# Moving the last transposes, loads and stores in the closing units of a conditioned attention + causal convolution kernel

## The chip, the cores and the metric

One core of one Trainium2 chip. The metric is device time in microseconds (us) of one execution; lower is better. TensorE (PE) does the matrix products and the transposes, VectorE (DVE) and ScalarE (ACT) read its results from PSUM, GpSimd (POOL) adds and reduces in SBUF, and SyncE (SP) issues every DMA of this kernel from one queue, in order.

## What is computed

The inputs are x of 4 x 1024 x 1024, four condition rows and the weights, all in f32. Cut to its core, the reference is:

```python
xn = rms_norm(x, g_norm) * (1 + scale) + shift      # scale, shift = cond @ W_emb + b_emb
q, k, v = split(xn @ W_qkv)                         # 16 heads of 64
q, k = rms_norm(q, g_q), rms_norm(k, g_k)
o = softmax(q @ k.T / 8) @ v
x = x + o + o @ W_out
x = x + causal_conv1d(x, 4 taps from cond) + b      # depthwise
```

## The kernel before, in words

**Stages.** The four batches are cut into 16 *doubles*, each two pairs of heads of one batch. A double's q, k and v come from 28 *products* (line 589; 4 matrix products of 128 x 384 each, counted twice for f32), seven block products P1 to P7 in Strassen's manner, for four token tiles each. Their operands are sums of blocks of the activations (`Chunk`, lines 257 to 329, written to scrA by way of the "r" buffers) and of the weights (`Weights`, lines 479 to 511, four blocks k = 0 to 3 for each double of weights, written to scrB by way of the "ob" buffers). A *unit* is one pair of heads and one half (512) of the query rows; there are 64, p = 0 to 63. Unit p scores eight key tiles (L629), copies them to SBUF (ScalarE, L637), keeps a running maximum (VectorE, L646), reduces it over the partitions (GpSimd, L651), copies it into PSUM (L660), subtracts it (VectorE, L665), takes the exponential (ScalarE, L669) and adds the rows (GpSimd, L671). The values' product (L692) and the row sums (`finish`, L707) of unit p - 1 are written between the scores of unit p. The row sums go through DRAM to be spread and inverted (`spread` L725 to 730, `invert` L733 to 738), and `divide` (L747) writes the output of the pair to scrO.

**What fills a unit.** Between its scores a unit runs other pieces: seven steps T = 7(p+4) to 7(p+4)+6 of the list of products, the transposes of q and k (`transposes`, L459, with the copies kT and qT, L465 and L467), and output products. `split` puts the last 26 us of pieces (20 in the first 16 units) behind the unit's maximum. Products end at T = 447, in unit 59. The output of batches 0 to 2 is done by 70 block products (`Quad`, L881), of which the last two, g = 68 and 69, lie in unit 59; eight outputs of batch 2 (`REST`) are done plainly (`Out`) in units 60, 61 and 62, three, three and two; 16 outputs of batch 3 are last, seven of them (`own`) behind the last unit's maximum. An output is a residual (four transposes, L936), two products (L950, k = 0 to 3 and 4 to 7), a copy and an activation on ScalarE (L960, L974), three taps on VectorE (L986), four transposes (L997), a copy (L1001) and a DMA (L1002). `gather` (L770) loads a half of a batch's attention output from scrO in two transfers.

**Order.** TensorE, VectorE, ScalarE and GpSimd execute in the order in which the program is written. SyncE's queue is ordered by the compiler, so that a load can be issued well ahead of its place. The program keeps a planned clock: every piece has a planned time, `tick` adds it, and steps given to `defer` are written when the planned clock reaches their due time. `defer_gap` gives a step to the gap after a maximum instead: 2.7 us after a unit's `softmax`, `fill_gap` writes up to 6.5 us of them, scales of q and k first. `defer_quiet` moves a step that would fall into the exponentials to their end. `need(key)` writes the steps of a key at once: the transposes need the scale of their q and k (L450, L451), `load_w` of a block with summed weights needs all of a double's `combine`, and a product with the output weights needs the addition of the identity to them (`diagonal`, L930).

**Buffers.** Tag "m" is three PSUM tiles, for all products, transposes and row sums. "ob" (2) holds the operands of output products, "r" (2) the chunks, "x" (6) x, y, ot and squares, "wo" (3) output weights. `late` is the list of outputs whose transposes are still to come, with the planned time at which each was appended; `store(age)` writes those that are at least `age` old.

```python
PRODUCTS order: P1,P2 (8 steps), P6 (8-11), P7 (12-15), P4 (16-19), P5 (20-23), P3 (24-27)
LEADS = ((11, 7), (10, 9))     # [pair][half]: transposes so many steps behind the block's last product
R_HOME = ("r", 8, 2)
```

Of the kernel before, what the change touches and what calls it, by code (L numbers as in the profile page):

```python
# [21 lines left out]
def kernel(  # L22
# [33 lines left out]
    B, N, DIM = x.shape  # L56
    D = DIM // HEADS
    NJ = DIM // P
# [33 lines left out]
    clock = [0.0]  # L92
# [164 lines left out]
    class Chunk:  # L257
# [69 lines left out]
        def store(self):  # L327
            for src, i0, i1 in self.stores:
                nc.sync.dma_start(scrA[self.b][self.q][:, i0:i1, self.k, :], src)
# [149 lines left out]
    class Weights:  # L479
# [6 lines left out]
        def load(self):  # L486
            d, k = self.d, self.k
            self.b = {}
            four = apool.tile([P, 4, HN], F32, tag="ob", name=f"b_{self.name}", bufs=2)
            for kh in range(2):  # L490
                for y in range(2):
                    t = four[:, 2 * kh + y, :]
                    self.b[kh, y] = t[:, :W3]
                    for s, src in enumerate(w_block(kh, 2 * d + y, k)):
                        nc.sync.dma_start(t[:, s * P : (s + 1) * P], src)
            if d:
                if d > 1:
                    defer_gap(5.0, ("B", d), 2.5, self.combine)
                else:
                    defer_quiet(TO_B, ("B", d), self.combine)  # L500
# [18 lines left out]
    NPR = len(PRODUCTS)  # L519
# [238 lines left out]
    def gather(b, half):  # L758

        for kh in range(2):  # L760

            n = KH - kh if b == B - 1 else KH
            for k in range(n):
                need("oT", b, kh * KH + k, half)
            if half and b == B - 1:
                four = apool.tile([P, 8, QN], F32, tag="r", name=f"ob_{b}_{kh}_{half}", bufs=2)
                four = four.rearrange("p i t -> p (i t)").rearrange("p (k t) -> p k t", t=HN)
            else:
                four = apool.tile([P, KH, HN], F32, tag="ob", name=f"ob_{b}_{kh}_{half}", bufs=2)
            nc.sync.dma_start(four[:, :n, :], scrO[b][half][:, kh * KH : kh * KH + n, :])  # L770
            for k in range(n):
                oTs[b, kh * KH + k, half] = four[:, k, :]
# [240 lines left out]
    BEHIND = 26  # L1013
    SHARES = (0.25, 0.5, 0.25)
    LEADS = ((11, 7), (10, 9))
    DIVIDE = 18.0
    STEP_FIRST = 1.6
    BEHIND_FIRST = 20.0
# [2 lines left out]
    AGE = 30.0  # L1021
    LOUD = 5.0
    AGE_REST = 5.0
    W_AT = 3
    STORE = 30.0
    TO_B = 12.0
    P6_AT = 3
    STEPS_B = ((16, 19, 22, 25), (7, 12, 17, 22))
    outs, norms, chunks, weights, doubles, quads = {}, {}, {}, {}, {}, {}
    LAST = (B - 1) * 2 * NJ  # L1030
    NB = 2 * NJ
    ND = B * NJ // 2
# [3 lines left out]
    def piece(T):  # L1036


        n, i = divmod(T, NPR)
        pieces = []  # L1040
        free = lambda f: pieces.append((0.0, f))
        if i == 0 and n < ND and n not in doubles:
            free(lambda: doubles.__setitem__(n, Double(n)))

        for m in (n, n + 1):
            for name, at in WEIGHTS.items():
                if m == 0:
                    at = WEIGHTS_FIRST.get(name, NPR)
                elif m == 1 and name == "P6":
                    at = P6_AT  # L1050
                if m < ND and at + (m - n) * NPR == i:
                    free(lambda m=m, name=name: load_w(m, name))
        a = T // 2 + LOADS_A
        if T % 2 == 0 and 4 <= a < ND * NPR // 2:
            free(lambda: load_a(a))

        for name, (c, g) in ENDS.items():
            last = max(j for j, pr in enumerate(PRODUCTS) if pr[0] == name)
            for s, at in ((1, last + LEADS[c][g]), (0, last + LEADS[c][g] + 1)):
                m = n - at // NPR  # L1060
                if i == at % NPR and 0 <= m < ND:
                    pieces.append((0.45, lambda m=m, s=s, c=c, g=g: doubles[m].pairs[c].transposes(g, s)))
        if n < ND:
            b, d = divmod(n, PB)

            if b + 1 < B and d == PB - 2:
                if i == 0:
                    norms[b + 1] = Norm(b + 1, range(NT))
                if i % 3 == 0 and i < 24:
                    free(lambda: norms[b + 1].squares(i // 3))  # L1070
                if i == 26:
                    free(norms[b + 1].root)
            if b + 1 < B and (d == PB - 1 or d == PB - 2 and i == 27):
                s = (i + 1) // 3
                if i == 27 and d == PB - 2:
                    free(lambda: chunk_load(b + 1, 0))
                elif i % 3 == 1 and i < 24:
                    s = i // 3
                    free(lambda: chunk_load(b + 1, s + 1))
                    for c in range(2):  # L1080
                        pieces.append((0.45, lambda c=c: chunks[b + 1, s].transposes(c)))

            if b == 0 and d + 1 < PB and i in STEPS_B[d > 0]:
                free(lambda: Weights(d + 1, STEPS_B[d > 0].index(i)).load())

            if n in (PB - 1, PB) and i % 14 == W_AT:
                free(lambda: OutWeights((n - PB + 1) * 2 + i // 14).load())
            pieces.append((TIME, lambda: doubles[n].piece(i)))
        return pieces
# [21 lines left out]
    def out_load(m):  # L1111
        if m < B * NB and m not in outs:
            b, i = divmod(m, NB)
            outs[m] = Out(b, i % NJ, i // NJ)
            outs[m].load()

    def out_pieces(m):

        return [
            (0.0, lambda: out_load(m)),  # L1120
            (0.45, lambda: outs[m].residual()),
            (0.0, lambda: out_next(m)),
            (3.5, lambda: outs[m].product(0)),
            (3.5, lambda: outs[m].product(1)),
        ]

    NQ = 2 * KH + KH // 2
    NG = NQ * len(OUT)
# [7 lines left out]
    REST = [(B - 2) * NB + h * NJ + j for h in range(2) for j in (2, 3, 6, 7)]  # L1136
    REST_PLAN = {p: n for p, n in zip(range(B * NB - 4, B * NB - 1), (3, 3, 2))}

    def out_load_product(g):
        b, i = divmod(g, 4 * len(OUT))  # L1140
        j, i = divmod(i, len(OUT))
        if g < NG:
            if i == 0:
                quads[b, j] = Quad(b, j)
            quads[b, j].load(OUT[i])

    def out_product(g):
        b, i = divmod(g, 4 * len(OUT))
        j, i = divmod(i, len(OUT))

        def step():
            if g == 0:
                out_load_product(0)
            quad = quads[b, j]
            quad.product(OUT[i])
            if OUT[i] in quad.outs:
                late.append((clock[0], quad.outs[OUT[i]].store))
            out_load_product(g + 1)

        pieces = [(3.95 if OUT[i] in ("P2", "P3", "P7", "P4") else 3.5, step)]  # L1160
        return [(0.0, lambda: store(AGE))] + pieces
# [7 lines left out]
    def between(p):  # L1169

        b, i = divmod(p, NB)
        slots = [[] for _ in range(7)]
        for j in range(7):
            T = 7 * (p + 4) + j
            slots[j] = piece(T) if T < ND * NPR + max(LEADS[1]) + 2 else []
        slots[0].append((0.0, lambda: store(AGE)))
        d, k = divmod(p - 11, NB)
        if 0 <= d < B - 1 and k % 2 == 0 and k < NJ:
            slots[0].append((0.0, lambda: OutSums(d, k // 2).load()))
        for a, g in enumerate(range(products_until(p), products_until(p + 1))):  # L1180
            slots[(2, 5)[a]] += out_product(g)
        if p in REST_PLAN:
            at = sum(n for q, n in REST_PLAN.items() if q < p)
            for m in REST[at : at + REST_PLAN[p]]:
                if m in REST[:: len(REST) // 2]:
                    slots[6].append((0.0, lambda m=m: gather(B - 2, m // NJ % 2)))
                slots[6] += [(0.0, lambda: store(AGE_REST))] + out_pieces(m)
                slots[6].append((0.0, lambda m=m: late.append((clock[0], outs[m].store))))
        return [piece for slot in slots for piece in slot]
# [12 lines left out]
    def run(pieces):  # L1202
        for t, step in pieces:
            until = clock[0] + t
            step()
            if until > clock[0]:
                tick(until - clock[0])
# [33 lines left out]

    own = []
    for m in range(LAST, LAST + NJ - 1):
        own += out_pieces(m) + [(0.45, store), (0.0, lambda m=m: late.append((clock[0], outs[m].store)))]

    last = None
    for p in range(B * NB):
# [34 lines left out]
    last.finish()  # L1282
    last.divide()
    for m in range(LAST + NJ - 1, B * NB):
        run(out_pieces(m) + [(0.45, store)])
        late.append((clock[0], outs[m].store))
    store()

# [37 lines left out]
```

## Time and profile before

| what | value |
|---|---|
| median of 3 runs | 2920.79 us (2920.69 to 2922.56) |
| the profiled run | 2919.7 us |
| its span, first to last instruction | 2917.7 us |
| mean granted TensorE clock | 0.987 |
| DMA | 510.98 MB, mean 175 GB/s; 53.3% of 16 engines' span |

The page has six parts: busy time by engine, the span in 40 slices, DMA queues, the chain of work that ended last, the costliest groups of instructions, and the DMA issues. A group's line gives the line of the program, the engine, the operation, out<-in by name with shapes, the count, the busy time with the mean of one, and the idle time just ahead with what released it. A timeline gives start, duration, and instructions that follow one another, merged; a bracket holds the idle time ahead and its releaser. f32 matrix products are recorded as two instructions each, and the ends of TensorE's instructions are modelled, so that a duration overlaps the next start by some tenths of a us; the steps between starts are the safer measure.

In the chain of the whole span TensorE has 71%, VectorE 13%, ScalarE 7%, DMA 4% and unexplained issue 3%. TensorE's share of busy time in the 40 slices is 90% or more in all but the first (7 tenths) and two late ones (8 tenths).

### The profile page before, as it was taken

How to read it: one execution, taken by the hardware profiler on the slowest of the kernel's cores; microseconds unless marked ns; L12 is line 12 of the kernel's file. 1: busy time of each engine (PE TensorE's matmuls, PEld its weight loads, DVE VectorE, ACT ScalarE, POOL GpSimd, SP SyncE). 2: the span in 40 equal slices, each digit the busy share in tenths (PEclk: the TensorE clock that was granted, in tenths of full speed). 3: DMA queues.
4: the chain of work that ended last, by engine and by line, in shares of the span. 5: the costliest groups of instructions: out<-in, count | busy, mean ns of one | idle time of the engine just before them, and what ended most of it. 6: DMA issues, size and time to landing. Idle time of an engine off the chain costs nothing.

```text
span 2917.7 us, 32188 instructions
## 1 busy us (share of the span) xinstructions
PE 2797.4 (96%) x10529; PEld 1322.4 (45%) x10529; DVE 2183.2 (75%) x2652; ACT 1692.7 (58%) x2269; POOL 1347.7 (46%) x534
## 2 busy tenths in 40 slices
PE   7999999999999999999999999999999999998999
PEld 3544444444444444454444444445444444443344
DVE  3578877888878767787878777787877777687653
ACT  3165757765656666764656667675555656565532
POOL 1045555555455553544554455355455544553520
PEclk9999999999999999999999999999999999999999
DMA  7864555645444555764565556656555444433333
GB/s 280 270 211 139 166 171 176 220 157 177 159 156 162 202 178 188 231 205 161 175 213 168 172 177 202 208 193 208 169 176 189 163 139 135 161 120 109 101 105 115
DMA packets 416254, 510.98 MB, mean 175 GB/s; under 512 B 41888, under 2 KB 327896, under 8 KB 406360
## 3 DMA queue, kind: packets, MB, share of 16 engines
q1 hardware_dynamic: 416088, 508.93, 53.3%
q8 instruction: 84, 1.38, 0.2%
q14 instruction: 82, 0.67, 0.1%
HBM read 413.43 MB, written 95.40 MB: 174 GB/s over the span
## 4 chain that ended last, share of the span: by engine, by line
PE 71%; DVE 13%; ACT 7%; DMA 4%; issue 3%; POOL 1%; SPq 1%; DVEq 0%; ACTq 0%; POOLq 0%
PE pqkv_P L589 28%; PE pav L692 14%; PE s L629 13%; PE po L950 5%; DVE mx L646 4%; PE po_P L881 4%; PE po L881 3%; ACT sp L637 3%; DVE sp L665 2%; ACT sp L669 1%; PE qkt L459 1%; DVE y L986 1%; PE tot L707 1%; DMA rec<-scrR 1%; PE otp L997 1%
## 5 line engine op out<-in xcount | busy, mean ns | idle before, releaser
L589 PE MATMUL pqkv_P<-w_P,a 128*128 128x384 f32 x3504 | 1198.5, 493 | 30.8 <-issue 12.0
L671 POOL TENSOR_TENSOR sum<-sum,sp 128x1024 f32<-128x1024 f32 x384 | 958.1, 2495 | 73.2 <-ACT sp L669 43.1
L589 PEld LDWEIGHTS pqkv_P<-w_P,a 128*128 128x128 f32 x3504 | 652.5, 192 | 505.7 <-issue 93.1
L637 ACT COPY sp<-s 128x1024 f32<-128x1024 f32 x512 | 512.0, 1015 | 486.9 <-PE s L629 380.8
L646 DVE TENSOR_TENSOR mx<-mx,sp 128x1024 f32<-128x1024 f32 x384 | 514.6, 1340 | 166.2 <-ACT sp L637 137.8
L665 DVE TENSOR_TENSOR sp<-sp,mbp 128x1024 f32<-128x1024 f32 x512 | 604.9, 1213 | 15.4 <-ACT mbp L660 15.1
L669 ACT ACTIVATE sp<-sp 128x1024 f32<-128x1024 f32 x512 | 526.7, 1054 | 138.8 <-DVE sp L665 134.6
L651 POOL PARTITION_ALL_REDUCE mb<-mx x64 | 221.4, 3459 | 828.2 <-DVE mx L646 559.3
L629 PE MATMUL s<-qT,kT 64*128 64x512 f32 x2048 | 518.6, 623 | 34.3 <-ACT sp L637 22.6
L692 PE MATMUL pav<-sp,v 128*64 128x512 f32 x2048 | 472.4, 604 | 0.7 <-DVE oT L747 0.7
L671 POOL TENSOR_TENSOR sum<-sp,sp 128x1024 f32<-128x1024 f32 x64 | 151.3, 2364 | 497.3 <-ACT sp L669 240.4
L629 PEld LDWEIGHTS s<-qT,kT 64*128 64x128 f32 x2048 | 170.0, 186 | 333.2 <-issue 172.3
L986 DVE SCALAR_TENSOR_TENSOR y<-x,cols,y 128x512 f32<-128x512 f32 x192 | 249.4, 1303 | 61.2 <-ACT y L974 56.6
L692 PEld LDWEIGHTS pav<-sp,v 128*64 128x64 f32 x2048 | 136.8, 138 | 322.3 <-issue 312.1
L646 DVE TENSOR_TENSOR mx<-sp,sp 128x1024 f32<-128x1024 f32 x64 | 107.8, 1685 | 103.7 <-ACT sp L637 103.7
L608 DVE TENSOR_TENSOR qk<-u,pqkv_P 128x256 f32<-128x256 f32 x256 | 106.8, 417 | 83.0 <-PE pqkv_P L589 81.0
L950 PE MATMUL po<-ob,wo 128*128 128x512 f32 x352 | 159.6, 606 | 4.4 <-DMA ob<-scrO 4.4
L881 PE MATMUL po_P<-o_P,wq_P 128*128 128x512 f32 x320 | 144.0, 592 | 0.2 <-DVE u L610 0.2
L660 ACT COPY mbp<-mb 128x1024 f32<-128x1024 f32 x64 | 65.1, 1018 | 118.3 <-POOL mb L651 118.2
L451 DVE TENSOR_TENSOR qk<-qk,ms 128x1024 f32<-128x1024 f32 x64 | 124.5, 1945 | 2.2
L881 PE MATMUL po<-o_P,wq_P 128*128 128x512 f32 x240 | 108.0, 592 | 0.0
L437 ACT ACTIVATE sq<-qk 128x512 f32<-128x512 f32 x128 | 76.6, 627 | 48.7 <-DVE qk L608 48.7
(96 smaller groups left out, 1890.5 us busy)
## 6 DMA issues: line engine op xcount, KB each, us to landing
a<-scrA SPq DMA_DIRECT2D x215, 512.0 KB
w_P<-scrB SPq DMA_DIRECT2D x64, 768.0 KB
o_P<-scrS SPq DMA_DIRECT2D x40, 1024.0 KB
w_P<-in_L_cond_W_qkv_dram SPq DMA_DIRECT2D x144, 256.0 KB
o_P<-scrO SPq DMA_DIRECT2D x30, 1024.0 KB
scrA<-r SPq DMA_DIRECT2D x28, 896.0 KB
wq_P<-scrW SPq DMA_DIRECT2D x70, 256.0 KB
xc<-in_x_dram SPq DMA_DIRECT2D x64, 256.0 KB
```

What stands on the lines that cost most here:

```text
L589: nc.tensor.matmul(pm, (chunks[0, k].r(place) if a is None else a[:, k, :])[:, t % 2 * P : (t % 2 + 1) * P], w[:, k, :], start=(k == 0), s ...
L629: nc.tensor.matmul(ps[:, h, :], pr.kT[kt // HT][h * D : (h + 1) * D, kt % HT * P : (kt % HT + 1) * P], pr.qT[self.half][h * D : (h + 1) * ...
L637: nc.scalar.copy(sp, ps)
L646: nc.vector.tensor_max(self.mx, self.mx if kt > 1 else self.sp[0], self.sp[kt])
L651: nc.gpsimd.partition_all_reduce(self.mb.rearrange("p h q -> p (h q)"), self.mx.rearrange("p h q -> p (h q)"), P, bass_isa.ReduceOp.max,)
L665: nc.vector.tensor_sub(self.sp[kt], self.sp[kt], self.mb)
L669: nc.scalar.activation(sp, sp, AF.Exp)
L671: nc.gpsimd.tensor_tensor(self.sum, self.sum if kt > 1 else self.sp[0], sp, ALU.add)
L692: nc.tensor.matmul(self.pav[h * D : (h + 1) * D, :], self.pr.v[kt // HT][:, kt % HT, h * D : (h + 1) * D], self.sp[kt][:, h, :], start=(kt ...
L881: nc.tensor.matmul(pm, self.w[name][:, k, :], self.o[name][:, k, :], start=(k == 0 and name not in ("P2", "P3", "P4")), stop=(k == KH - 1),)
L950: nc.tensor.matmul(self.pm, self.w[kh][:, k % KH, :], oTs[b, k, half], start=False, stop=(k == NJ - 1),)
L986: nc.vector.scalar_tensor_tensor(self.y, self.x1[:, k : k + HN], cols[:, r : r + 1], self.y, ALU.mult, ALU.add)
```

## The change

It has four parts.

1. *First weights' sums.* For the second double of weights (d = 1), `combine` of blocks k = 2 and 3 is given to `defer_gap` (2.5 us each) instead of `defer_quiet` with 12 us. The loads of blocks 0 and 1 come at steps 14 and 17 of the first double instead of 16 and 19.
2. *Last pair's transposes.* For the last double alone (m = ND - 1), the transposes of the second pair's second half (after P5) come 12 steps behind the block, not 9: T = 455 and 456, slots 0 and 1 of unit 61, instead of T = 452 and 453, slots 4 and 5 of unit 60. The other leads are the same, and the limit of T becomes 464.
3. *Attention output.* The second half of batch 2, like that of batch 3, is loaded into the "r" buffers instead of "ob". Both halves' `gather` calls for batch 2, and the load of the first `REST` output, are written after product g = 69 in unit 59, instead of in units 60 and 61 ahead of the outputs that use them.
4. *Outputs' transposes.* In `own` and in the last loop, `store` takes only outputs at least 8.5 us old on the planned clock, where one output adds 7.45: an output's transposes are written after the second output behind it, not the first. The planned 0.45 of that piece is gone.
Apart from these, the loop over `s` and `m` in `piece` is another way to write the same leads.

```diff
             if d:
-                if d > 1:
+                if d > 1 or k > 1:
                     defer_gap(5.0, ("B", d), 2.5, self.combine)
                 else:
                     defer_quiet(TO_B, ("B", d), self.combine)
...
-            if half and b == B - 1:
+            if half:
                 four = apool.tile([P, 8, QN], F32, tag="r", name=f"ob_{b}_{kh}_{half}", bufs=2)
...
+    LEADS_LAST = ((11, 7), (10, 12))
...
+    AGE_OWN = 8.5
...
-    STEPS_B = ((16, 19, 22, 25), (7, 12, 17, 22))
+    STEPS_B = ((14, 17, 22, 25), (7, 12, 17, 22))
...
-            for s, at in ((1, last + LEADS[c][g]), (0, last + LEADS[c][g] + 1)):
-                m = n - at // NPR
-                if i == at % NPR and 0 <= m < ND:
-                    pieces.append((0.45, lambda m=m, s=s, c=c, g=g: doubles[m].pairs[c].transposes(g, s)))
+            for s in (1, 0):
+                for m in (n - 1, n):
+                    at = last + (LEADS_LAST if m == ND - 1 else LEADS)[c][g] + 1 - s
+                    if 0 <= m < ND and (n - m) * NPR + i == at:
+                        pieces.append((0.45, lambda m=m, s=s, c=c, g=g: doubles[m].pairs[c].transposes(g, s)))
...
             out_load_product(g + 1)
+            if g == NG - 1:
+                for half in range(2):
+                    gather(B - 2, half)
+                out_load(REST[0])
...
-            slots[j] = piece(T) if T < ND * NPR + max(LEADS[1]) + 2 else []
+            slots[j] = piece(T) if T < ND * NPR + 16 else []
...
-                if m in REST[:: len(REST) // 2]:
-                    slots[6].append((0.0, lambda m=m: gather(B - 2, m // NJ % 2)))
...
-        own += out_pieces(m) + [(0.45, store), (0.0, lambda m=m: late.append((clock[0], outs[m].store)))]
+        own += out_pieces(m) + [(0.0, lambda: store(AGE_OWN)), (0.0, lambda m=m: late.append((clock[0], outs[m].store)))]
...
-        run(out_pieces(m) + [(0.45, store)])
+        run(out_pieces(m) + [(0.0, lambda: store(AGE_OWN))])
         late.append((clock[0], outs[m].store))
```

## The prediction, made before the changed kernel was run

> **What bounds the kernel now.** I read the page first (shares, then the chain that ended last), then TensorE's timeline at both ends of the span, then VectorE's, ScalarE's, GpSimd's and SyncE's timelines around each gap found there.
>
> ```profile
> PE 2797.4 (96%) x10529; PEld 1322.4 (45%) x10529; DVE 2183.2 (75%) x2652; ACT 1692.7 (58%) x2269; POOL 1347.7 (46%) x534
> ```
>
> TensorE sets the time, so an edit is worth what it takes out of, or puts into, TensorE's gaps and slow stretches. TensorE's timeline over the last 300 us, columns start, duration, what, and in brackets the idle time ahead with its releaser:
>
> ```profile
> 2630.85 0.66 PE L997 MATMUL otp<-ident,y 128*128 128x128 f32 x4
> 2637.41 1.97 PE L459 MATMUL qkt<-ident,qk 128*128 128x128 f32 x8 [5.90 <-DVE qk L451]
> 2639.17 1.06 PE L997 MATMUL otp<-ident,y 128*128 128x128 f32 x4
> 2640.02 1.06 PE L936 MATMUL po<-ident,xc 128*128 128x128 f32 x4
> 2640.87 7.74 PE L950 MATMUL po<-ob,wo 128*128 128x512 f32 x16
> 2648.45 0.60 PE L936 MATMUL po<-ident,xc 128*128 128x128 f32 x4
> 2648.89 7.03 PE L950 MATMUL po<-ob,wo 128*128 128x512 f32 x16
> ...
> 2689.38 0.60 PE L936 MATMUL po<-ident,xc 128*128 128x128 f32 x4
> 2694.33 10.09 PE L950 MATMUL po<-ob,wo 128*128 128x512 f32 x16 [4.35 <-DMA ob<-scrO]
> ...
> 2806.16 1.09 PE L997 MATMUL otp<-ident,y 128*128 128x128 f32 x4 [3.52 <-DVE y L986]
> 2807.04 1.06 PE L936 MATMUL po<-ident,xc 128*128 128x128 f32 x4
> 2807.89 7.00 PE L950 MATMUL po<-ob,wo 128*128 128x512 f32 x14
> ```
>
> See three waits, each followed by work slower than its like: 8 transposes in 1.97 us (1.09 elsewhere), an output's product in 7.74 or 10.09 (7.03). The first waits for VectorE:
>
> ```profile
> 2628.07 7.86 DVE L646 TENSOR_TENSOR mx<-mx,sp 128x1024 f32<-128x1024 f32 x6
> 2635.85 0.25 DVE L450 RECIPROCAL ms<-ms 128x16 f32<-128x16 f32 x1
> 2636.13 1.23 DVE L451 TENSOR_TENSOR qk<-qk,ms 128x1024 f32<-128x1024 f32 x1
> ```
>
> The scale that the transposes force stands behind the unit's maxima. The fourth gap is in unit 0, on TensorE and then on VectorE:
>
> ```profile
> 162.72 0.60 PE L459 MATMUL qkt<-ident,qk 128*128 128x128 f32 x4
> 169.19 5.43 PE L589 MATMUL pqkv_P<-w_P,a 128*128 128x384 f32 x8 [5.86 <-issue]
> ```
>
> ```profile
> 150.12 0.56 DVE L510 TENSOR_TENSOR b<-b 128x384 f32<-128x384 f32 x1 [0.83 <-DMA b<-in_L_cond_W_qkv_dram]
> 152.54 1.74 DVE L510 TENSOR_TENSOR b<-b 128x384 f32<-128x384 f32 x3 [1.86 <-DMA b<-in_L_cond_W_qkv_dram]
> 154.20 3.88 DVE L646 TENSOR_TENSOR mx<-mx,sp 128x1024 f32<-128x1024 f32 x3
> ```
>
> "Issue" at 163 names no releaser; TensorE resumes at 169.19, just as VectorE ends the adds of product 30 (168.47 to 169.09), which free one of the three PSUM tiles "m". They stand behind the first shift, that behind the spread maximum (GpSimd 161.95 to 166.26, ScalarE's copy to 167.31), that behind the maxima, and those behind the sums of the fourth weight block, which wait for their DMA.
>
> **What the skill says.** "TensorE: Matmul & The Clock Gate", Part 1: an idle window of about 3.4 us halves TensorE's clock. Agrees: 8 transposes took 1.97 us after 5.90 idle and 1.09 otherwise, and a 1.75 us wait (at 95 us) shows no slowing. "SBUF — State Buffer", Who interferes with whom: a VectorE operation with two SBUF inputs and a GpSimd one that reads SBUF shut each other out. Agrees: three taps took 7.46 us beside GpSimd's sums, 2.33 alone. The clock page, Architectural detail: VectorE and ScalarE are strict FIFO; the queue behind the maxima above is that.
>
> **The change, part by part.**
>
> (1) First weights' sums. Blocks 2 and 3 of the second pair of heads' weights (4 subtractions each, 2.33 us) leave the scores' stretch for the gap after the maximum; the loads of blocks 0 and 1 start two products (5.2 us) sooner. Without the sums the maxima are bound by ScalarE's last copy (154.05) and VectorE: seven maxima of 1.24 and two reductions (1.27) from 146.73, with the waits for copies, end at 156.7, not 161.65. GpSimd 3.25 to 4.3, the copy 1.0: spread at 162. But VectorE now has 2 x 2.33 of sums, 1.5 of scale and up to 1.3 of waiting for GpSimd's port ahead of the shift: 156.7 + 7.5 = 164.2, not 167.34, so 3.1 sooner (4.4 without port waiting). TensorE's wait shrinks to about 3 us or less and perhaps its slow product (5.43 for 2.75) goes too; that would be 5.7 or more, but GpSimd's sums, which end at 192.85 just ahead of the row sums at 193.50, move by 3 to 4 only and cap it. **-3.5**; ends 0 and -8.5 (5.86 + 2.6). The stores and the load of w that follows them come some 8 us later on SP's queue; the load of a behind it lands near 171 for a use at 172, so it is just hidden; uncovered it costs about 1.
>
> (2) Last pair's transposes. Eight move from unit 60 to unit 61, their scale into unit 60's gap (1.5 us of VectorE, which is nearly idle from 2641 to 2650: free). From 2631.51 to the end of the first rest output at 2648.45 are 16.94 us; left are 0.44 + 0.44 + 6.87 = 7.75 (steps of the warm outputs). **-9.2**. What else it needs by then: y of the last product's output (taps end 2625.75) is ready; its w diagonal (2637.27 in VectorE's order) and x (issued 2634.03) are late for 2632, but part 3 loads that output in unit 59, so both move ahead of the maxima. Unit 60's later chain (copy of the maximum, shifts, exps, sums) hangs on this product's end through ScalarE's order and shifts with it. In unit 61 sixteen transposes stand in a row, then two outputs' transposes and a residual: seven PSUM tiles through three buffers at ScalarE's 0.53 to 0.59 a copy. The residual starts near 2683.1 instead of 2682.03: **+1.1**. New order: with 0.9 less on the planner's clock, the reciprocal of the row sums (L733) falls behind the first rest output's taps, as it does in unit 62 (2739.92): about 3 us later in its chain. Row reciprocals then land near 2650 for a division near 2651: hidden, 0 to +3.
>
> (3) Attention output. The second half of batch 2 gets the "r" buffers, idle since batch 3's chunks, instead of waiting for "ob". Its two 1 MB transfers leave 2687 to 2694, so 4.35 + (10.09 - 7.03) = **-7.4**. Next late is the next output's diagonal, behind taps and four shifts on VectorE: +0.2 to +0.5. I take **-7.2**. Batch 3's second half now waits for "r" until the last rest output (2740 and 2743.5), batch 3's first half can go into "ob" at 2686: at 2741 one 1 MB transfer, not 1.8 MB, runs beside the rec transfer (7.34 us) that the unit 63 stall hangs on: **-0.8**, ends -4 and +2 (a SyncE queue held longer by it).
>
> (4) Outputs' transposes. From 2802.5 to 2815.59 are 13.1 us where a warm step is 7.75: **-5.3**. One output later y is 7.4 us older (taps end 2806.0, next use 2809.9). At the end, one output's four transposes leave the last product's front for the wait on the last taps: **-0.4**. The "x" ring of 6 then holds y of three outputs, one ot and at most two x: just enough.
>
> Sum: -3.5 - 9.2 + 1.1 - 7.2 - 0.8 - 5.3 - 0.4 = **-25.3**. The profiled run took 2919.7 (span 2917.7 and 2.0 around it): 2894.4. The median stands 1.1 above it: **2895.5**.
>
> **Rivals.** (a) A new wait in unit 60 (chance 0.16): the late reciprocal holds SyncE's queue, the weights of the second rest output queue behind it, and its second product waits 4 us and runs cold, or unit 0 gives nothing. Of part 2 some 2 are left, or of part 1 none: 2899 to 2903. For it: in unit 60 SyncE now issues those weights (2645.70) right behind rec. Against: in unit 62, with that order, the weights went ahead. (b) More than I count (0.15): unit 0's whole stall, and rec no longer disturbed, its row sums' wait (1.96) gone: 2888 to 2891. (c) **Slower** (0.05): the second half's data is whole by about 1820, and batch 3's chunks still write "r" until 1934. If SyncE takes a buffer as soon as it is free (a transfer of batch 3 was issued at 2487.99, 255 us ahead of its place), the chunks have one buffer. One at 1851 holds it until its store at 1879, the next came at 1865: 14 us of wait and 3 cold; two such meetings are 34: 2895.5 + 34 = 2929. It decides from 25 us on. Against: x loads (2560.96, 2600.64) did not overtake tiles that engines write in their ring, while w loads, with a ring of their own, did. (d) The change doesn't act (0.04), TensorE's gaps being filled by others behind them: 2916 to 2921.
>
> **Numbers.** 2895.5 within 2891 and 2899: 0.60. Low 2889, high 2906, from the parts' ends and case (a). What a measurement here can tell from no change is about 0.2%, 5.8 us: below 2915 is faster. Faster 0.91, same 0.04, slower 0.05.
>
> **What would show it.** No wait on qk L451 and no DMA ob wait on TensorE; rest outputs at 7.03 each; no wait on y L986 but the last; sixteen qkt in unit 61; the wait at 163 at 3 us or less. Wrong if the rest outputs wait for wo, if chunks' transposes wait near 1860, or if row sums wait for GpSimd.

## The result, and the profile after

| what | before | after |
|---|---|---|
| median on the first chip, 6 runs each | 2919.65 us (2914.30 to 2922.56) | 2900.64 us (2891.97 to 2907.69) |
| ratio, with its 95% interval | 1 | 0.9937 (0.9915 to 0.9959) |
| median on a later chip, 11 and 6 runs | 2915.35 us (2909.45 to 2922.58) | 2895.52 us (2891.95 to 2900.84) |
| ratio there | 1 | 0.9933 (0.9918 to 0.9947) |
| the profiled run | 2919.7 us | 2907.69 us |
| its span | 2917.7 us | 2905.7 us |

The change is faster by some 18 to 20 us; the second interval is 15.5 to 23.9 us (0.0053 and 0.0082 of 2915). Predicted were 25.3 us less and a time of 2895.5. The profiled run of the first set was the slowest of its six, so its span is not compared as a whole below, but stage by stage.

**TensorE's timeline of the kernel after**, units 60 and 61, columns as before:

```profile
2636.72 0.64 PE L707 MATMUL tot<-sum,ones 128*32 128x256 f32 x8
2639.20 1.09 PE L997 MATMUL otp<-ident,y 128*128 128x128 f32 x8
2640.13 0.60 PE L936 MATMUL po<-ident,xc 128*128 128x128 f32 x4
2640.57 7.03 PE L950 MATMUL po<-ob,wo 128*128 128x512 f32 x16
...
2655.62 7.03 PE L950 MATMUL po<-ob,wo 128*128 128x512 f32 x16
2664.88 1.13 PE L629 MATMUL s<-qT,kT 64*128 64x512 f32 x4 [1.17 <-DVE sp L665]
...
2680.05 1.53 PE L459 MATMUL qkt<-ident,qk 128*128 128x128 f32 x12
2682.21 0.66 PE L459 MATMUL qkt<-ident,qk 128*128 128x128 f32 x4 [0.63 <-ACT kT L465]
...
2691.55 7.03 PE L950 MATMUL po<-ob,wo 128*128 128x512 f32 x16
```

The wait of 5.90 us for the scale and that of 4.35 us for "ob" are gone, and the rest outputs' products take 7.03 us (one, at 2699.29, 7.22). From the first transpose (2639.20) to the end of the third product's steps (2662.58, where a step is 6.96 as at 2730.97 to 2737.93) are 23.4 us, 32.7 before: the predicted 9.2 are there. One wait is new: the second pair of scores waits for VectorE's last shift. VectorE's timeline of the kernel after says why:

```profile
2662.47 1.23 DVE L930 TENSOR_TENSOR wo<-wo,ident 128x128 f32<-128x128 f32 x1 [2.26 <-DMA scrO<-oT]
2663.62 1.21 DVE L665 TENSOR_TENSOR sp<-sp,mbp 128x1024 f32<-128x1024 f32 x1
```

The shift stood behind the addition of the identity to the weights of the fourth rest output, ahead of which VectorE was idle for 2.26 us. This output is not used before unit 61. The addition waited for its weights: their load was issued at 2659.25, and the last wait on a semaphore ahead of it ended at 2662.4. (The bracket names another transfer; in the kernel with part 2 and the early load, below, it names the weights.) VectorE's timeline of the kernel before has the same addition behind the last shift, where nothing waited for it:

```profile
2661.10 2.34 DVE L665 TENSOR_TENSOR sp<-sp,mbp 128x1024 f32<-128x1024 f32 x2
2663.36 2.38 DVE L930 TENSOR_TENSOR wo<-wo,ident 128x128 f32<-128x128 f32 x1
```

The load was issued equally far ahead of the end of the third product in both kernels (3.3 us: 2660.26 of 2663.59, 2659.25 of 2662.58). So what changed is the place of the addition in VectorE's order, which follows the planned clock.

The first gap, in unit 0, is smaller but not gone. TensorE, then VectorE of the kernel after:

```profile
167.45 5.46 PE L589 MATMUL pqkv_P<-w_P,a 128*128 128x384 f32 x8 [3.23 <-issue]
```

```profile
158.11 6.15 DVE L510 TENSOR_TENSOR b<-b 128x384 f32<-128x384 f32 x8
164.18 0.25 DVE L450 RECIPROCAL ms<-ms 128x16 f32<-128x16 f32 x1
164.46 1.22 DVE L451 TENSOR_TENSOR qk<-qk,ms 128x1024 f32<-128x1024 f32 x1
165.61 1.21 DVE L665 TENSOR_TENSOR sp<-sp,mbp 128x1024 f32<-128x1024 f32 x1
```

The spread maximum was in PSUM at 162.83 (ScalarE's copy, 161.81 and 1.02 long). The shift began at 165.61, since the sums and the scale stood ahead of it: 2.8 us that the part costs itself.

At the end only the last four transposes still wait for their taps, as predicted, but twelve transposes now stand behind the last product, not eight, and eight in a row stand behind the first output of that stretch:

```profile
2834.22 1.04 PE L997 MATMUL otp<-ident,y 128*128 128x128 f32 x8
2835.75 0.66 PE L936 MATMUL po<-ident,xc 128*128 128x128 f32 x4 [0.48 <-ACT y L974]
...
2896.87 1.04 PE L997 MATMUL otp<-ident,y 128*128 128x128 f32 x8
2900.84 1.09 PE L997 MATMUL otp<-ident,y 128*128 128x128 f32 x4 [2.94 <-DVE y L986]
```

To count stage by stage I use the starts of the row sums (L707) of each unit on TensorE as marks: in the table and wherever a unit's time is given below, "unit 60" is from the row sums of unit 59 to those of unit 60, and so on; "end" is what follows those of unit 63. The same marks serve for all kernels below; times in us, each from one profile.

| kernel | start to the row sums of unit 1 | units 2 to 58 | 59 | 60 | 61 | 62 | 63 | end | 59 to end |
|---|---|---|---|---|---|---|---|---|---|
| before | 229.3 | 2354.7 | 44.3 | 48.5 | 48.6 | 40.6 | 72.6 | 79.1 | 333.6 |
| after | 227.6 | 2365.8 | 43.3 | 40.8 | 42.2 | 39.2 | 66.9 | 79.8 | 312.3 |
| after, second set | 228.7 | 2357.2 | 43.8 | 40.7 | 42.5 | 39.4 | 66.9 | 79.8 | 313.0 |
| part 1 alone | 224.9 | 2350.5 | 43.3 | 49.1 | 49.0 | 40.6 | 72.6 | 79.1 | 333.7 |
| parts 2 to 4 | 230.8 | 2354.4 | 43.2 | 41.1 | 42.3 | 39.2 | 66.8 | 79.8 | 312.4 |
| part 2 alone | 231.0 | 2353.9 | 43.3 | 51.0 | 46.4 | 40.0 | 73.9 | 78.7 | 333.3 |
| part 2 and the early output load | 229.1 | 2356.5 | 43.8 | 40.9 | 45.1 | 40.0 | 73.9 | 78.7 | 322.4 |
| parts 2 and 3 | 228.5 | 2352.9 | 43.2 | 40.8 | 42.3 | 39.7 | 73.0 | 79.1 | 318.0 |
| part 3 alone | 228.8 | 2355.2 | 43.4 | 49.0 | 41.1 | 39.2 | 73.7 | 78.9 | 325.2 |
| part 4 alone | 228.7 | 2351.3 | 43.7 | 49.1 | 46.6 | 40.0 | 66.8 | 79.4 | 325.7 |
| after, one sum in the gap | 224.9 | 2361.7 | 43.2 | 40.9 | 42.1 | 40.4 | 67.1 | 79.4 | 313.0 |
| after, reciprocal sooner | 226.9 | 2351.9 | 43.2 | 40.8 | 42.5 | 40.8 | 67.2 | 79.4 | 313.8 |
| after, both of these | 224.3 | 2357.7 | 43.2 | 41.2 | 42.2 | 39.6 | 66.9 | 79.4 | 312.3 |
| after, diagonal later | 226.3 | 2352.4 | 43.2 | 39.4 | 42.7 | 40.5 | 67.2 | 79.4 | 312.3 |

The closing stage (59 to the end) is 20.6 to 21.3 us shorter. The trace's sums over it, by windows, say of what kind the gain is (columns: window, length, busy us of PE, PEld, DVE, ACT and POOL with their instructions, granted clock, DMA share, GB/s). After, then before:

```profile
2593.00:2906.00 313.00, 294.82 (x1040) 133.72 (x1036) 208.90 (x219) 139.77 (x215) 106.42 (x40) 0.99 0.37 111
```

```profile
2584.00:2918.00 334.00, 302.83 (x1038) 138.37 (x1036) 208.20 (x219) 139.68 (x215) 106.05 (x40) 0.96 0.35 107
```

Of the 21 us, 13 are idle time (334 - 302.83 = 31.2 against 18.2) and 8 are busy time for the same work: the work behind the waits that are gone no longer runs slow. The granted clock went from 0.96 to 0.99.

### The profile page after: what moved, and what is told of

Its sections match the earlier page's. It is cut to its first block, busy times and chain, and to the rows that moved or that the text cites. A ratio compares the mean times of both kernels' runs of the same rounds, so it can differ in the third digit from the quotient of the medians.

```text
span 2905.7 us, 32179 instructions
## 1 busy us (share of the span) xinstructions
PE 2793.5 (96%) x10529; PEld 1317.5 (45%) x10529; DVE 2182.2 (75%) x2652; ACT 1695.1 (58%) x2269; POOL 1345.1 (46%) x534
## 4 chain that ended last, share of the span: by engine, by line
PE 69%; DVE 14%; ACT 7%; DMA 5%; issue 3%; POOL 1%; SPq 1%; DVEq 0%; ACTq 0%; POOLq 0%
PE pqkv_P L589 27%; PE pav L692 14%; PE s L629 13%; PE po L950 5%; DVE mx L646 5%; PE po_P L881 4%; PE po L881 3%; ACT sp L637 3%; DVE sp L665 3%; ACT sp L669 2%; DMA scrR<-few 1%; DMA rec<-scrR 1%; DVE r L321 1%; PE qkt L459 1%; PE tot L707 1%
## 5 line engine op out<-in xcount | busy, mean ns | idle before, releaser
L986 DVE SCALAR_TENSOR_TENSOR y<-x,cols,y 128x512 f32<-128x512 f32 x192 | 248.0, 1296 | 46.8 <-ACT y L974 42.2
```

What stands on the lines that cost most here:

```text
L986: nc.vector.scalar_tensor_tensor(self.y, self.x1[:, k : k + HN], cols[:, r : r + 1], self.y, ALU.mult, ALU.add)
```

## The experiments

### Part 1 alone, and parts 2 to 4 without it

The kernel before with only these lines; the other kernel is the changed one with these lines taken back.

```diff
-                if d > 1:
+                if d > 1 or k > 1:
...
-    STEPS_B = ((16, 19, 22, 25), (7, 12, 17, 22))
+    STEPS_B = ((14, 17, 22, 25), (7, 12, 17, 22))
```

> The kernel before with part 1 alone (sums of weight blocks 2 and 3 in the gap, first loads two steps sooner). My theory, corrected by the profile after: product 32's wait falls from 5.86 to about 3.2 us and its product stays slow (5.4), because the eight subtractions stand ahead of the first shift; from the start of unit 0's scores to its row sums 47.6 us instead of 49.9, so 2 us in all, and nothing after unit 1 changes, since every queue has the old order there. Rival A (the whole stall was bought): wait under 1, product 2.75, 5 or more. Rival B (the middle of the kernel, which was 10.7 us longer in the profile after between the row sums of units 1 and 58, was lengthened by these loads): units 2 to 16 longer by 7 here and not in the kernel with the other parts alone.

> The changed kernel without part 1. My theory: from the row sums of unit 58 to the end as in the kernel after (some 312.3 us against 333.6 before, 21 less), unit 0 as before (wait 5.86), so about 2 us slower than the whole change and some 19 to 21 faster than before. Rival B: if part 1's loads lengthen the middle, this kernel is 5 or more faster than the whole change.

Part 1 alone: 2910.66 us (12 runs) against 2913.36 (15 runs), ratio 0.9987 (0.9975 to 0.9998), so 0.6 to 7.3 us faster. Parts 2 to 4: 2895.1 us (4 runs), ratio 0.9940 (0.9919 to 0.9961) to the same runs of before. Their closing stage is that of the whole change (312.4), and part 1's is that of before (333.7): the two do not touch one another. TensorE of the kernel with part 1 alone has the same wait in unit 0 as the whole change, and yet a product at full speed behind it:

```profile
167.34 2.82 PE L589 MATMUL pqkv_P<-w_P,a 128*128 128x384 f32 x8 [3.21 <-issue]
189.04 0.64 PE L707 MATMUL tot<-sum,ones 128*32 128x256 f32 x8
```

2.82 here, 5.46 in the kernel after. My expectation had this product slow.

What part 1 gives in one execution hangs on this. From unit 0's first scores to its row sums, so that what scatters ahead of unit 0 is left out, were 49.9 us before (48.5 to 49.9 in the seven profiles without part 1). In the five with part 1 unaltered they are 47.6, 47.5, 46.3, 46.1 and 44.6 us, in just the order of this product's times: 5.46, 5.46, 4.43, 4.30 and 2.82.

### Part 4 alone

```diff
-        own += out_pieces(m) + [(0.45, store), ...
+        own += out_pieces(m) + [(0.0, lambda: store(AGE_OWN)), ...
...
-        run(out_pieces(m) + [(0.45, store)])
+        run(out_pieces(m) + [(0.0, lambda: store(AGE_OWN))])
```

> The kernel before with part 4 alone (an output's transposes one output later). My theory: the wait on y L986 at the fourth output of batch 3 goes and with it the slow output behind it, 5.3 us between the row sums of units 62 and 63, and 0.4 more that returns after the row sums; units 59 to 62 as before. Rival: the wait only moves to another output or into the ring of x (a wait of ScalarE on a buffer), less than 2 us gained.

One run, 2907.58 us. Unit 63 is 5.7 us shorter (66.8 for 72.6), the end 0.4 longer. Its units 61 and 62 were shorter too, by 2.0 and 0.6, though the edit touches nothing in them: TensorE's wait for "ob" was 3.66 us there and the product behind it took 8.83, where the kernel before has 4.35 and 10.09. Part 2 alone shows nearly the same 46.4 and 40.0, so a stage of one profile can be off by 2 us.

### Part 2 alone, with the early load, and with the whole of part 3

Part 2 is the LEADS_LAST lines and the new loop over `s` and `m`. The second kernel adds only this to it; the third adds all of part 3.

```diff
             out_load_product(g + 1)
+            if g == NG - 1:
+                out_load(REST[0])
```

> The kernel before with part 2 alone (eight transposes of q and k from unit 60 to unit 61), the first rest output loaded where it was. My theory: the wait on qk goes, but the diagonal of the first rest output's weights, written at its product and so behind all maxima and now the scales on VectorE, is late next: TensorE waits until 2637 to 2639 on the old clock for wo L930 and runs cold, so only 1 to 2 us are gained from unit 59's row sums to unit 60's, and 1.1 are lost in unit 61. Rival: the first rest output follows at once and the whole 9 us come from this part.

> Part 2 with nothing of part 3 but the early load of the first rest output (its x and weights asked for behind the last block product); the attention output stays in the buffers of before. Alone, part 2 gained nothing: TensorE's wait of 5.90 for VectorE's scale became one of 5.15 for the x of that output. If that load was all that stood in the way, unit 60 has no wait ahead of its rest outputs and takes 41 to 42 us (51.0 with part 2 alone, 48.5 before), unit 61 still waits for the attention output: 46 to 49. If the loads of the attention output hold it up too, since they stand ahead of it in SyncE's queue, unit 60 keeps 3 us or more of wait and takes 44 to 51.

> Parts 2 and 3 without 1 and 4. If the parts add up once 2 has its load, units 60 and 61 take 83 us together (97.1 before, 97.4 with part 2 alone, 90.1 with part 3 alone), unit 63 still 72.6 to 74 us, and from the row sums of unit 58 to the end 317 to 320 us (333.6 before, 312.3 with all parts). If the outputs' transposes were needed for it, units 60 and 61 take 86 us or more.

Alone, part 2 gained nothing (one run, 2920.13 us): unit 60 took 51.0 us, 48.5 before. TensorE of that kernel:

```profile
2636.92 1.08 PE L936 MATMUL po<-ident,xc 128*128 128x128 f32 x4 [5.15 <-DMA xc<-in_x_dram]
```

The wait for the scale was replaced by one for the x of the first rest output, whose load had had that long to arrive before. My expectation had named this output's weights, not its x. The new wait for VectorE's last shift is there too, 2.29 us long. With this output's load asked for a unit sooner and nothing else of part 3 (2909.83 us, one run), the wait for x is gone, and what is left in unit 61 is the wait for the attention output:

```profile
2631.89 1.09 PE L997 MATMUL otp<-ident,y 128*128 128x128 f32 x8
2632.82 0.60 PE L936 MATMUL po<-ident,xc 128*128 128x128 f32 x4
2633.26 7.03 PE L950 MATMUL po<-ob,wo 128*128 128x512 f32 x16
...
2687.19 7.13 PE L950 MATMUL po<-ob,wo 128*128 128x512 f32 x16 [2.75 <-DMA ob<-scrO]
```

Unit 60 is then 40.9 us, the whole change's. With all of part 3 (2901.31 us, one run) units 60 and 61 take 83.1 us together, as in the whole change. So the theory holds: the attention output's loads ahead of it in SyncE's queue did not hold up the x load, and the outputs' transposes of part 4 are not needed for part 2.

### Part 3 alone

```diff
-            if half and b == B - 1:
+            if half:
...
+            if g == NG - 1:
+                for half in range(2):
+                    gather(B - 2, half)
+                out_load(REST[0])
```

> The kernel before with part 3 alone (batch 2's second half in the r buffers, both halves and the first rest output loaded in unit 59). My theory: the 4.35 us wait for ob and the slow product behind it go, 7 us between the row sums of units 60 and 61; unit 60 keeps its wait of 5.9 on qk, and the first row of unit 63's stall changes by 1 us or less. Rival: the transfers only collide elsewhere, at the place where they are now issued (near 1940 and 2176), and give back more than 2 us there.

One run, 2911.16 us: unit 61 is 7.5 us shorter (41.1), unit 62 1.4 shorter (39.2). Unit 63 is 1.1 longer, and this need not be part 3's doing: behind the same wait of 3.5 us for the taps, the product with "ob" took 8.13 us, 7.00 before. Parts 2 and 3 alone gain 0.3 and 8.4 us in the closing stage, together 15.6: 7 us are there only when both are.

### One of the two sums in unit 0's gap

```diff
-            defer(TO_MAX + 0.1, key, lambda: fill_gap(GAP))
+            defer(TO_MAX + 0.1, key, lambda: fill_gap(GAP if self.name != "0_0_0" else 3.0))
```

> The changed kernel with only one of the two weight blocks' sums in the gap of unit 0's maximum; the other is written where the summed weights are needed, behind the first shift and the adds of product 30. My theory (product 32 waits for VectorE's queue ahead of the first shift): its wait falls by the 2.3 to 2.8 us of four subtractions, from 3.2 to under 1, and its product runs at 2.75 instead of 5.46; the row sums of unit 0, which GpSimd's additions bound, come 1 to 3 us sooner, not 5. Rival: the wait stays near 3 us, because the copy of the maximum (ends 162.8) and not the subtractions decides.

2895.72 us (4 runs), ratio 0.9935 (0.9911 to 0.9959). VectorE, then TensorE of this kernel:

```profile
158.04 3.91 DVE L510 TENSOR_TENSOR b<-b 128x384 f32<-128x384 f32 x4
161.87 0.25 DVE L450 RECIPROCAL ms<-ms 128x16 f32<-128x16 f32 x1
162.15 1.23 DVE L451 TENSOR_TENSOR qk<-qk,ms 128x1024 f32<-128x1024 f32 x1
163.29 1.21 DVE L665 TENSOR_TENSOR sp<-sp,mbp 128x1024 f32<-128x1024 f32 x1
164.42 0.41 DVE L608 TENSOR_TENSOR qk<-u,pqkv_P 128x256 f32<-128x256 f32 x1
164.75 0.28 DVE L608 TENSOR_TENSOR v<-u,pqkv_P 128x128 f32<-128x128 f32 x1
164.95 2.33 DVE L510 TENSOR_TENSOR b<-b 128x384 f32<-128x384 f32 x4
```

```profile
165.14 2.82 PE L589 MATMUL pqkv_P<-w_P,a 128*128 128x384 f32 x8 [0.99 <-PE qkt L459]
169.09 0.63 PE L459 MATMUL qkt<-ident,qk 128*128 128x128 f32 x4 [1.13 <-DVE v L608]
```

With four subtractions instead of eight ahead of it, the first shift starts 2.3 us sooner, the wait is 0.99 us, and the product is at full speed; unit 0's row sums start at 188.85 (192.11 in the kernel after). This shows that TensorE waited for VectorE's queue ahead of the first shift; the rest of the prediction's chain (shift, adds, PSUM tile) is read from the lines, where TensorE starts at 165.14, just as the adds end. The four subtractions beside GpSimd's maximum (158.35 to 161.71) took 3.91 us, the four after it 2.33. The Trainium skill, "SBUF — State Buffer", Who interferes with whom, has a VectorE operation with two inputs in SBUF contend with a GpSimd one that reads SBUF, and this agrees. The 3 us gained in unit 0 cannot be seen in the median.

### The reciprocal of the row sums sooner

```diff
-            defer(8.0, key, self.invert)
+            defer(5.5 if b == B - 1 and self.half and c > NJ - 4 else 8.0, key, self.invert)
```

> The changed kernel with the reciprocal of the row sums (L733) written 2.5 us sooner in units 60 and 62, so that VectorE does it ahead of the rest output's taps, not behind them. My theory: the rec transfer lands 2 to 3 us sooner, so that VectorE's 2.2 us wait for it ahead of oT in unit 63 goes; TensorE's 3.1 wait for a score's copy stays (that copy is bound by the exponentials ahead of it on ScalarE), but the row sums' wait of 2.5 for GpSimd shrinks to under 1: 1 to 3 us less between the row sums of units 61 and 62. Unit 60 does not change, its 1.2 us wait being on a weights' diagonal. Rival: nothing changes, because the rec transfer waits for the 1 MB transfer issued beside it, not for its own start.

2894.53 us (4 runs), ratio 0.9929 (0.9905 to 0.9953). The division no longer waits for its rec transfer (2.23 us in the kernel after), but the row sums wait the longer. TensorE, then GpSimd of this kernel:

```profile
2728.61 3.65 PE L692 MATMUL pav<-sp,v 128*64 128x512 f32 x16
...
2745.98 1.73 PE L707 MATMUL tot<-sum,ones 128*32 128x512 f32 x8 [4.80 <-POOL sum L671]
```

```profile
2725.50 2.36 POOL L671 TENSOR_TENSOR sum<-sp,sp 128x1024 f32<-128x1024 f32 x1 [7.31 <-ACT y L974]
2727.94 17.99 POOL L671 TENSOR_TENSOR sum<-sum,sp 128x1024 f32<-128x1024 f32 x6
```

GpSimd's seven sums ran without a pause up to the row sums, so that the next bound there is GpSimd: the wait for it took 4.80 us instead of 2.54, and unit 62 as a whole 40.8 instead of 39.2. The values' product took 3.65 us instead of 5.35. Both stand behind a wait of 3.1 us ahead of the scores, which the edit left as it was, so that the product at full speed need not be the edit's doing. Nothing is gained in the closing stage (313.8).

### Both of these, beside the changed kernel as it is

The kernel "both" has the two edits just shown; the other is the changed kernel, unaltered, on the same chip.

> The changed kernel with two small edits: one of the two weight sums alone in unit 0's gap, and the reciprocal of the row sums 2.5 us sooner in the closing units. If both act, unit 0's row sums start near 189 (192.1 in the changed kernel) and the median is 3 to 4 us under the changed kernel run beside it. If the closing edit only moves the wait from the division to the row sums' wait for GpSimd, as its own run showed (4.80 in place of 2.54 us there), only unit 0's 3 us are left, which is about what the scatter of runs hides: 0 to 3 us under.

> The changed kernel unaltered, beside the kernel before on the same chip, to settle its middle: between the row sums of units 1 and 58 nothing of its order of instructions differs from the kernel before, yet its first profiled run had 2365.8 us there against 2354.7. If that is a scatter of single executions, this profile has 2350 to 2357 us there and the median lies 20 to 25 us under the kernel before, with row sums of unit 58 to the end at 312 to 313. If the change itself slows the middle (blocks of weights summed later, loads at other times), the middle is again 2362 us or more and the median again only 15 to 19 us under.

2895.77 us and 2895.52 us (6 runs each), ratios to before 0.9932 (0.9913 to 0.9950) and 0.9933 (0.9918 to 0.9947): no difference, though the row sums of unit 1 came 4.4 us sooner in the one profile (224.3 to 228.7; 3.2 us of this lie ahead of unit 0's scores). The second profile of the changed kernel has 2357.2 us in units 2 to 58, neither clearly among the 2350 to 2357 of one theory nor at the 2362 of the other; the median lies at the edge of what scatter alone would give (19.8 under before, 20 to 25 expected). Undecided.

### The fourth rest output's diagonal later

```diff
-            defer(4.5, ("wo", self.name), self.diagonal)
+            defer(14.0 if (self.b, self.half, self.j) == (B - 2, 0, 7) else 4.5, ("wo", self.name), self.diagonal)
```

> The changed kernel, with the addition of the identity to the weights of the fourth rest output planned 14 us behind their load instead of 4.5, so that it no longer stands ahead of unit 60's last shift on VectorE. If the new wait of 1.17 to 1.7 us there is the whole reason why unit 60 gave back part of what its transposes freed (7.7 us gained of 9.4), the wait before the second pair of scores goes and unit 60 takes 39 to 39.6 us, from the row sums of unit 58 to the end 311 to 312 (40.7 to 41.2 and 312.3 to 313.9 with the change as it is). If scores there wait for the shift's successor all the same (the exponential, a copy on ScalarE, GpSimd's sums), unit 60 keeps 40.5 us or more, or unit 61 gives it back.

2891.6 us (4 runs) against 2919.57, ratio 0.9904 (0.9877 to 0.9930). TensorE of this kernel, the scores that waited:

```profile
2647.75 1.99 PE L629 MATMUL s<-qT,kT 64*128 64x512 f32 x8
2649.67 3.65 PE L692 MATMUL pav<-sp,v 128*64 128x512 f32 x16
```

No wait, and unit 60 takes 39.4 us: the new wait did hang on that one addition, and with it gone the stage has 9.1 us less than before. But unit 62 is 1.3 us longer than in the kernel after, and the closing stage as a whole is the same 312.3. There the row sums of units 61 and 62 now waited 0.56 and 2.95 us for GpSimd, none and 2.54 in the kernel after. This kernel has the lowest median of all, though in a set of its own; its closing stage does not explain it, so the edit is not shown to be the reason.

## Why the prediction was right, and where it was off

The direction and, in the main, the mechanism of each part were right. The time was predicted as 2895.5; the medians were 2900.6 and 2895.5. That the second is met to the digit is luck: on that chip the kernel before took 2915.4, not the 2920.8 from which the prediction counted down, and the difference was predicted some 5 to 6 us too large, just outside both intervals. By the terms of the sum:

| term | predicted | measured | from |
|---|---|---|---|
| unit 0's sums | -3.5 (0 to -8.5) | -2.6 (-0.8 to -4.6) | row sums of unit 1: mean of five profiles with part 1 unaltered, 226.9; of seven without it, 229.5 (from unit 0's first scores to its row sums, 46.4 and 49.3) |
| unit 60's transposes | -9.2 | -7.7 | 48.5 to 40.8 |
| sixteen transposes in unit 61 | +1.1 | +1.2 | parts 2 and 3 against part 3 alone, 42.3 and 41.1 |
| attention output | -7.2 | -7.5 (-5.5 from part 4 alone's 46.6) | part 3 alone, unit 61 |
| rec beside one transfer | -0.8 | -1.4 | unit 62, 40.6 to 39.2 |
| outputs' transposes | -5.3 | -5.7 | part 4 alone, unit 63 |
| the tail | -0.4 | +0.7 | end, 79.1 to 79.8 |
| sum | -25.3 | -23.0 | |

**Unit 0.** Right in its chain, and the shift came when it said but for a start 1.4 us later: maxima to 158.11 (156.7 predicted; unit 0's first scores began 0.9 later in this profile, 144.49 for 143.60), then 7.5 us to the shift at 165.61, as predicted. The wait became 3.23 us ("about 3"). What the step could not say is whether the product behind it runs slow: after waits of 3.20 to 3.23 us, it took 2.82, 4.30, 4.43, 5.46 and 5.46 us in five profiles. The Trainium skill, "TensorE: Matmul & The Clock Gate", Part 1, has the clock decided over free-running windows of about 3.4 us, so that the outcome depends on where the wait falls in them. The scatter of these five fits that, though no run here shows the windows themselves. The stated length does not fit as it stands: waits recorded as 3.2 us were enough, and the last section has a shorter one.

**Unit 60.** The working from the first transpose to the outputs' end was right to 0.2 us. The step that failed is that unit 60's later chain "hangs on this product's end through ScalarE's order and shifts with it": in VectorE's part of that chain the fourth output's identity addition moved from behind the last shift to ahead of it, and its weights came no sooner ahead of the product's end than before. The prediction had seen such a move for the reciprocal, by the planned clock, but not for this addition. This new wait took back 1.2 us as recorded, 1.4 to 1.7 in the stage; the diagonal experiment showed the place. Rival (a), a new wait in unit 60, was right in its kind and wrong in its mechanism: SyncE issued the second output's weights at 2644.20, ahead of the row sums' inverse at 2651.41, and no product waited for weights. The reciprocal did fall behind the taps (2651.18) and was hidden, as predicted.

**The load in unit 59.** The prediction said that without part 3 the x of the first rest output would be late. That is what part 2 alone showed: 5.15 us of wait, and a gain of nothing.

**Attention output, rec, outputs.** All three within 0.6 us in the table, the first only to the 2 us by which unit 61 scatters without it. For rec the mechanism holds only in part: its division waited 2.23 us instead of 3.61, and the values' product lost its own wait (0.68 us) and 0.6 us of slow time, but GpSimd took half of that back (row sums' wait 2.54, 1.96 before). The other 0.7 us of the 1.4 was not counted at all: behind the same wait of 3.1 us, the four score instructions ahead of that product took 1.13 us, 1.81 before. Behind this wait (3.1 to 3.4 us), scores and product together took 7.6 to 7.8 us in all five profiles without part 3 and 6.4 to 6.5 in eight of the nine with it (4.8, their full speed, with the reciprocal sooner); why the slow stretch is shorter is open.

**The tail.** The prediction counted what the last transposes lose in front of the last product, not what was moved to it. An output's four transposes (0.44 us) left unit 63, which is the 0.4 more that unit 63 gained, and came into the end; and eight transposes in a row ahead of a residual brought a wait for ScalarE in the PSUM ring, 0.48 us.

**Rival (c), slower,** did not come about: the two loads of the second half were issued at 1939.98, between the last two stores of chunks (1929.30 and 1943.28), and at 2175.86. The first took the buffer that the last chunk but one had left, the last chunk kept the other: the ring went by the order of the program, and no transfer took a buffer from a chunk. The prediction's "whole by about 1820" holds for the first transfer alone, four pairs (the last of them stored at 1822.57); the second could not have met the chunks, since its last pair was stored at 2167.80. **Rivals (b) and (d)** fell with the table: no term gave much more than counted, and the gaps did close.

**What stays open.** The terms sum to -23.0; the medians differ by -19.0 and -19.8. The rest would lie in units 2 to 58, where every engine has the same instructions in the same order, but for the two loads of the attention output and two neighbouring loads that changed places on SyncE's queue. There seven profiles without part 1 have 2351.3 to 2356.5 us (mean 2354.1) and seven with it 2350.5 to 2365.8 (mean 2356.7). What differs is small waits in changing places; of the waits for VectorE's shifts, the kernel after, then before:

```profile
PE s L629 <- DVE sp L665: 13.8, 9, 3.4
```

```profile
PE s L629 <- DVE sp L665: 11.4, 6, 2.8
```

The columns are us in total, times and the longest. The kernel with part 1 alone, which has the shortest middle of all, has 12.5 us in 7 of them. That part 1 itself costs 2 to 3 us there is neither shown nor excluded.

## What to carry to other kernels

When a wait is taken away, list every input of the next instruction and when each was asked for: here the transposes moved in vain until one output's loads (its x of 0.25 MB was what TensorE waited for) were asked for a unit sooner, and two parts worth 0.3 and 8.4 us alone were worth 15.6 together. Read what is queued on the in-order engine between the freed work and its next user, for an operation there with slack of its own (the identity addition) can wait on a DMA and stop what has none. A gap on the bounding engine costs its length and the slow time after it. In unit 0 these were 8.5 us (a wait of 5.86, and 5.43 for a product of 2.75); cutting the wait to 3.2 us left 3.3 to 5.9 of them, cutting it to 1 us left 1.1.

## What the runs showed of the hardware that was not expected

- After waits of 3.20 to 3.23 us a product of 2.75 us took 2.82 to 5.46 us, in the same program order. After waits of 4.41 to 5.88 us it took 4.67 to 5.46 us in the seven profiles without part 1. The slow stretch can outlast the wait: behind the 4.35 us for "ob" in the kernel before, the product's first seven instructions started 0.79 to 1.01 us apart, the other nine 0.43, so that some 6 us ran at about half speed.
- A shorter wait can be followed by slow work too. With part 2 alone, scores of 1.13 us took 2.01 behind a wait of 2.29 us, and an output's product of 7.03 us took 8.76 behind one of 2.46; with the early load it took 7.13 behind one of 2.75. TensorE of the kernel with part 2 alone:

```profile
2661.44 1.13 PE L629 MATMUL s<-qT,kT 64*128 64x512 f32 x4
2664.87 2.01 PE L629 MATMUL s<-qT,kT 64*128 64x512 f32 x4 [2.29 <-DVE sp L665]
```

- Single executions of one kernel on one chip differ by 8 to 16 us in sets of six and more (after: 2891.97 to 2907.69), and units 2 to 58, with the same order on the engines, by up to 15 us in 2355 between the profiles of the kernels shown, with no single wait to show for it.
